# Layer 2 of a four-layer image network: the scan's states in PSUM, its decays in SBUF

## The chip, the cores and the metric

The kernel runs on one core of a Trainium2 chip. The metric is device time in microseconds: 3410.98, the median of three runs (3406.53 to 3415.37). A change of about 0.3% (10 us) is the least that such runs can tell from none.

## The reference, cut to what matters

Four layers follow each other on four images of 128 channels and 64 x 64 pixels: attention (layer 0), two quantized 3 x 3 convolutions (layer 1), a selective scan (layer 2) and a second attention (layer 3). The change lies in layer 2, whose core is this recurrence over the 4096 pixels of an image:

```python
def step(h, inp):
    dt_t, B_t, C_t, x_t = inp
    dA = jnp.exp(dt_t[..., None] * A)
    dBx = dt_t[..., None] * B_t[:, None, :] * x_t[..., None]
    h = dA * h + dBx
    y = jnp.einsum('bdn,bn->bd', h, C_t)
    return (h, y)
```

There are 256 inner channels d and 16 states n per channel. B and C are shared by all channels, A is fixed for each channel and state. Afterwards y is multiplied by silu(z), brought back to 128 channels, normalized in groups, passed through silu and added to the input of the layer.

## The kernel before, in words

**Tiles and steps.** Channels lie on the 128 partitions, 256 of them as two halves. Pixels are taken in blocks of 512 (TB), eight blocks an image, so NG = 32 groups g in all. A group has 16 steps, one for each state n; a step is m = 16 g + n, and there are NM = 512. One step works on [128, 2, 512] float32 values:

- `fetches` (line 1080): SP loads bc, the rows of B and C for this state, spread over all partitions; three buffers, so it waits for the product with C three steps before.
- `decays` (line 1093, two chains, one a half): ScalarE computes da = exp(dt * A), 128 x 512, into one PSUM bank a half (tags da0 and da1 of the pool `ps_a`). Each has one buffer, so it waits for the scan that read the last one.
- `scans` (line 1119): VectorE multiplies ud = dt * x with B into hs (line 1126), then multiplies the hs of the step before, in place, with C (`readout`, lines 1114 to 1117, called at line 1131), then scans the two halves of hs in place (line 1134).
- `lasts` (line 1104): ScalarE copies the last column of hs to hlast (line 1109), from which the same state of the next block starts. The last of an image's eight groups has no such copy, so there are 448 of them.
- `additions` (line 1146): GpSimd adds hs to y (line 1151), and after the 16th step multiplies y with silu(z) (line 1155).

hs has three buffers in SBUF (line 1125). The two weight tiles of layer 1 use the same buffers at the start (line 289).

**Beside layer 2.** `preparation` makes dt, ud, x and silu(z) for a group (its VectorE instructions are at lines 982 to 990); `output` finishes a group and an image (statistics at line 1020); `convolutions` is layer 1 (VectorE at lines 804, 816, 833, 838 and 840). Both attentions are staged over four images: `energies`, `exponentials` and `products` keep TensorE and ScalarE at work during the scans; `high_low` (line 445), `finish0` (lines 694 and 705) and `finish3` (lines 735 and 765) have their VectorE work. In the last stage, layer 3 of the fourth image, when the scans are over, the sums of the attention's exponentials are formed by `accumulations` on VectorE (line 575) and `totals` on TensorE (line 578), which takes the two da banks in turn.

**What sets the order.** Nothing is scheduled by a compiler. Each function above is a generator that yields a planned operation (engine, planned duration, names of the marks it needs) and then issues its instructions. `Order.run` (line 115) takes, at each turn, the operation with the smallest planned start plus 0.15 times its rank from the table `RANKS` (line 52). `port=True` marks VectorE operations that the planner keeps apart from GpSimd's. The result is a fixed order on each engine and queue. The waits between engines do not come from the planner: the tile layer adds the semaphores that the use of the buffers asks for, on the instruction itself or, where there are several, as semaphore instructions ahead of it.

Of the kernel before, what the change touches and what calls it, by code (L numbers as in the profile page):

```python
# [8 lines left out]
F32 = mybir.dt.float32  # L9
# [11 lines left out]
P = 128  # L21
W = 64
N = W * W
TB = 512
NTB = N // TB
# [11 lines left out]
CB = 256  # L37
# [12 lines left out]


RANKS = {
    "layer1_weights": dict(SP=-5.3, ACT=9.6, DVE=17.6, PE=-7.5),
    "layer2_weights": dict(SP=11.2, ACT=5.6, DVE=13.0),
    "parts": dict(ACT=0.8),
    "first": dict(ACT=-1.6, DVE=-2.8, PE=-4.9),
    "convolutions": dict(ACT=2.0, DVE=4.4, PE=4.2),
    "preparation": dict(SP=16.0, PE=2.4, ACT=0.9, DVE=3.0),
    "output": dict(PE=3.0, ACT=0.0, DVE=1.7, SP=-3.8),
    "lasts": dict(ACT=-0.0),  # L60
    "energies": dict(PE=3.5),
    "exponentials": dict(ACT=1.4),
    "products": dict(PE=5.1),
    "decays": dict(ACT=0.8),
    "scans": dict(DVE=4.7),
    "additions": dict(POOL=9.6),
    "fetches": dict(SP=-17.0),
    "accumulations": dict(DVE=15.7),
    "totals": dict(PE=-1.0),
    "images": dict(SP=9.9),  # L70
    "high_low": dict(ACT=4.8, DVE=2.3),
    "copy": dict(ACT=2.5),
    "finish0": dict(DVE=2.9, ACT=-1.9, PE=-5.1),
    "stage_input": dict(SP=9.0),
    "residual": dict(SP=2.8),
    "finish3": dict(PE=4.1, DVE=3.8, ACT=3.2, SP=-14.6),
}


class Order:  # L80
# [25 lines left out]
    def mark(self, *key):  # L106
        self.marks[key] = self.end
# [70 lines left out]
def conv_seq_kernel(ctx: ExitStack, tc: tile.TileContext, i: dict, out: bass.AP):  # L178
    nc = tc.nc
# [106 lines left out]
    def layer1_weights(k):  # L286
        unit, dt = ((LEVELS, F32R), (LEVELS * LEVELS, FP8))[k - 1]
        yield op("SP", 0.3, lag=4.0)
        w = mam.tile([P, 2, TB], F32, tag="hs", name=f"w{k}", bufs=3)
        last = att.tile([P, TB], F32, tag="t", name=f"w{k}_8", bufs=1)[:, 0:P]  # L290
        ws = (flat(w), last)
        nc.sync.dma_start(out=ws[0], in_=i[f"L1_conv_w{k}T"][:, 0 : 8 * P])
        nc.sync.dma_start(out=ws[1], in_=i[f"L1_conv_w{k}T"][:, 8 * P : 9 * P])
        yield op("ACT", 1.3, table="exp")
        for t in ws:
            nc.scalar.activation(t, t, AF.Tanh)
        yield op("DVE", 1.4)
        mx = sml.tile([P, 2], F32, tag="wmx", name="wmx")
        for n, t in enumerate(ws):
            nc.vector.tensor_reduce(  # L300
                mx[:, n : n + 1], t, AX.X, ALU.max, apply_absolute_value=True
            )
        nc.vector.tensor_reduce(mx[:, 0:1], mx, AX.X, ALU.max)
        yield op("PE", 0.4, bank=True)
        pt = gtile("wmx_t")
        nc.tensor.transpose(pt[0:1, 0:P], mx[:, 0:1], ident)
        yield op("DVE", 0.3)
        m1 = sml.tile([1, 1], F32, tag="wm1", name="wm1")
        nc.vector.tensor_reduce(m1, pt[0:1, 0:P], AX.X, ALU.max)
        release()  # L310
        yield op("PE", 0.6, bank=True)
        pb = gtile("wmx_b")
        nc.tensor.matmul(pb[:, 0:1], lhsT=ones[0:1, :], rhs=m1, start=True, stop=True)
        yield op("DVE", 0.4)
        rec = sml.tile([P, 1], F32, tag="wrec", name="wrec")
        nc.vector.tensor_scalar_mul(rec, pb[:, 0:1], 2.0)
        release()
        nc.vector.reciprocal(rec, rec)
        yield op("DVE", 2.4)
        for t in ws:  # L320
            nc.vector.tensor_scalar(t, t, rec, 0.5, ALU.mult, ALU.add)
            nc.vector.tensor_scalar(t, t, LEVELS, MAGIC, ALU.mult, ALU.add)
            nc.vector.tensor_scalar(t, t, MAGIC, 2.0, ALU.subtract, ALU.mult)
        yield op("DVE", 1.1)
        wi = const.tile([P, len(TAPS), P], dt, tag=f"wint{k}", name=f"wint{k}")
        for n, (dy, dx) in enumerate(TAPS):
            t = 3 * dy + dx
            nc.vector.tensor_scalar_add(
                wi[:, n, :], ws[t // 8][:, t % 8 * P : (t % 8 + 1) * P], -LEVELS, saturate=False
            )  # L330
        wint.append(wi)
        yield op("ACT", 0.9, table="sqrt")
        s = const.tile([P, 1], F32, tag=f"bn_s{k}", name=f"bn_s{k}")
        sh = const.tile([P, 1], F32, tag=f"bn_b{k}", name=f"bn_b{k}")
        rsqrt(s, cols[f"L1_conv_var{k}"])
        yield op("DVE", 1.3)
        nc.vector.tensor_mul(s, s, cols[f"L1_conv_gamma{k}"])
        nc.vector.tensor_mul(sh, cols[f"L1_conv_mean{k}"], s)
        nc.vector.tensor_sub(sh, cols[f"L1_conv_beta{k}"], sh)
        nc.vector.tensor_scalar_mul(s, s, LEVELS / unit)  # L340
        nc.vector.tensor_scalar_mul(sh, sh, LEVELS)
        bn.append((s, sh))
        mark("w", k)
        if k == 1:
            order.add(layer1_weights(2))
# [43 lines left out]
        stages += [(3, b)] + ([(0, b + 3)] if b + 3 < B else [])  # L389
    NQ = NJ // 8  # L390
    NS = NCB * NQ
    accs, sss = {}, {}
    its, jts, vts, es, ps, uss = {}, {}, {}, {}, {}, {}

    def stage_input(s):
# [182 lines left out]
    def totals():  # L578
        mark("total", (len(stages) - 1) * NCB - 1)
        for k in range((len(stages) - 1) * NCB, len(stages) * NCB):  # L580
            need = [("da", NM - 1, h) for h in range(2)]
            if k >= (len(stages) - 1) * NCB + 2:
                need.append(("evicted", k - 2))
            yield op("PE", 0.45, ("acc", NQ * k + NQ - 1), *need, tiles="columns")
            sss[k] = ss = ps_a.tile([P, TB], F32, tag=f"da{k % 2}", name="ss", bufs=1)[:, 0:CB]
            acc = accs.pop(k)
            for m in range(4):
                nc.tensor.matmul(
                    ss[32 * m : 32 * m + 32, :],
                    lhsT=ones[:, 0:32],  # L590
                    rhs=acc[:, m % 2, m // 2, :],
                    start=True,
                    stop=True,
                )
            mark("total", k)
# [267 lines left out]
    NG = NTB * B  # L863
    NM = NG * DS
    hlast = mam.tile([P, DS, 2], F32, tag="hlast", name="hlast")
    stats, live, bcs, das, hss = {}, {}, {}, {}, {}

    def pair(name, tag, bufs):
        return mam.tile([P, 2, TB], F32, tag=tag, name=name, bufs=bufs)
# [223 lines left out]
    def decays(h):  # L1093
        for m in range(NM):
            g, n = divmod(m, DS)
            need = [("s", m - 1, h)] if m else []
            yield op("ACT", 0.7, ("dt", g), *need, table="exp")
            das[m, h] = da = ps_a.tile([P, TB], F32, tag=f"da{h}", name="da", bufs=1)
            nc.scalar.activation(  # L1099
                da, live["in", g][0][:, h, :], AF.Exp, scale=amat[:, h, n : n + 1]  # L1100
            )
            mark("da", m, h)

    def lasts():
        for m in range(NM):
            g, n = divmod(m, DS)
            if g % NTB < NTB - 1:
                yield op("ACT", 0.2, ("s", m, 1))
                nc.scalar.copy(hlast[:, n, :], hss[m][:, :, TB - 1])  # L1109
                mark("last", m)  # L1110
            else:
                order.known(0.0, "last", m)

    def readout(m):
        hs = hss[m]
        nc.vector.tensor_mul(hs, hs, bcs.pop(m)[:, 1:2, :].to_broadcast([P, 2, TB]))  # L1116
        mark("c", m)

    def scans():
        for m in range(NM):  # L1120
            g, n = divmod(m, DS)
            need = [("add", m - 3)] if m > 2 else []
            yield op("DVE", 1.2, ("bc", m), ("ud", g), *need, port=True)
            ud = live["in", g][1]
            hss[m] = hs = pair("hs", "hs", 3)
            nc.vector.tensor_mul(hs, ud, bcs[m][:, 0:1, :].to_broadcast([P, 2, TB]))  # L1126
            if n == 0:
                mark("begun", g)
            if m:
                yield op("DVE", 1.13, ("last", m - 1), port=True)  # L1130
                readout(m - 1)
            for h in range(2):
                yield op("DVE", 1.19, ("da", m, h))
                nc.vector.tensor_tensor_scan(  # L1134
                    hs[:, h, :],
                    das.pop((m, h)),
                    hs[:, h, :],
                    hlast[:, n, h : h + 1] if g % NTB else 0.0,
                    ALU.mult,
                    ALU.add,  # L1140
                )
                mark("s", m, h)
        yield op("DVE", 1.13, ("last", NM - 1), port=True)
        readout(NM - 1)

    def additions():
        for m in range(NM):
# [541 lines left out]
```

## Time and profile before

| What | Before |
|---|---|
| Median of three runs | 3410.98 us |
| The profiled execution: its time, its span | 3404.14 us, 3402.3 us |
| TensorE matmul, busy | 3123.7 us, 92% |
| VectorE, busy | 3024.0 us, 89% |
| ScalarE, busy | 2573.9 us, 76% |
| GpSimd, busy | 1319.4 us, 39% |
| 500 to 1000 us: VectorE, TensorE, ScalarE busy | 491.45, 462.64, 402.65 us |
| 2000 to 2500 us: the same | 486.45, 456.03, 394.07 us |
| 3000 to 3402 us: the same | 226.96, 380.55, 221.73 us |
| Copies to hlast, line 1109, ScalarE | 448 of 189 ns |
| Decays, line 1099, ScalarE | 1024 of 690 ns |

A row of the profile's list of groups names the line, the engine, the operation, the tile written and the tiles read, the shapes and the count; then the busy time in us and the mean of one instruction in ns; then the idle time of that engine just before these instructions, and what ended it. In the list of slices, each digit is the busy share of a fortieth of the span, in tenths. A timeline line gives the start and duration in us first, and in brackets an idle time before it with the instruction that ended it. [...]

### The profile page before, as it was taken

How to read it: one execution, taken by the hardware profiler on the slowest of the kernel's cores; microseconds unless marked ns; L12 is line 12 of the kernel's file. 1: busy time of each engine (PE TensorE's matmuls, PEld its weight loads, DVE VectorE, ACT ScalarE, POOL GpSimd, SP SyncE). 2: the span in 40 equal slices, each digit the busy share in tenths (PEclk: the TensorE clock that was granted, in tenths of full speed). 3: DMA queues.
4: the chain of work that ended last, by engine and by line, in shares of the span. 5: the costliest groups of instructions: out<-in, count | busy, mean ns of one | idle time of the engine just before them, and what ended most of it. 6: DMA issues, size and time to landing. Idle time of an engine off the chain costs nothing.

```text
span 3402.3 us, 69611 instructions
## 1 busy us (share of the span) xinstructions
PE 3123.7 (92%) x29359; PEld 2249.8 (66%) x29359; DVE 3024.0 (89%) x2828; ACT 2573.9 (76%) x3899; POOL 1319.4 (39%) x565
## 2 busy tenths in 40 slices
PE   7999989999889999998988999999899899998998
PEld 5887768788678776555547888755455455555665
DVE  3199999999999999999999999999999999994554
ACT  4588877878788786878777888877788787865554
POOL 0044444444334444444434444444444445441000
PEclk9999999999999999999999999999999999999999
DMA  3033343333443334444443333444444444330000
GB/s 80 23 97 101 89 121 97 98 101 98 111 111 101 97 94 125 105 110 109 111 138 97 97 91 93 120 97 110 124 111 108 130 104 116 105 111 18 8 11 12
DMA packets 194179, 321.72 MB, mean 95 GB/s; under 512 B 44352, under 2 KB 46784, under 8 KB 193856
## 3 DMA queue, kind: packets, MB, share of 16 engines
q1 hardware_dynamic: 193568, 316.32, 35.1%
q8 instruction: 232, 3.80, 0.4%
q10 hardware_dynamic: 288, 0.85, 0.1%
q14 instruction: 91, 0.75, 0.1%
HBM read 300.35 MB, written 16.78 MB: 93 GB/s over the span
## 4 chain that ended last, share of the span: by engine, by line
DVE 50%; PE 29%; issue 10%; ACT 9%; DMA 2%; SPq 0%; DVEq 0%; ACTq 0%
DVE hs L1134 21%; DVE hs L1126 12%; DVE hs L1116 9%; PE e L535 8%; PE us L624 6%; PE us L615 6%; ACT p L553 2%; ACT da L1099 2%; PE us L643 1%; DMA bc<-bc_d 1%; DVE ud L984 1%; PE proj L458 1%; PE proj L500 1%; PE conv L777 1%; ACT L1099 1%
## 5 line engine op out<-in xcount | busy, mean ns | idle before, releaser
L1151 POOL TENSOR_TENSOR y<-y,hs 128x1024 f32<-128x1024 f32 x512 | 1216.7, 2376 | 1751.3 <-DVE hs L1116 1699.0
L553 ACT ACTIVATE p<-e 128x1024 f32<-128x1024 f32 x1024 | 1011.3, 1017 | 186.1 <-PE e L535 86.5
L1134 DVE TENSOR_TENSOR_SCAN hs<-da,hlast,hs 128x512 f32<-128x512 f32 x896 | 1098.8, 1263 | 8.2 <-ACT da L1099 8.1
L615 PE MATMUL us<-v,p 128*128 128x129 f32 x8192 | 1028.7, 281 | 16.4 <-ACT us L671 16.4
L615 PEld LDWEIGHTS us<-v,p 128*128 128x128 f32 x8192 | 959.6, 193 | 79.1 <-ACT us L671 22.7
L1099 ACT ACTIVATE da<-dt,late 128x512 f32<-128x512 f32 x1024 | 701.5, 690 | 249.8 <-DVE hs L1134 247.0
L1116 DVE TENSOR_TENSOR hs<-hs,bc 128x1024 f32<-128x1024 f32 x512 | 674.0, 1316 | 20.7 <-ACT hlast L1109 20.5
L1126 DVE TENSOR_TENSOR hs<-ud,bc 128x1024 f32<-128x1024 f32 x512 | 661.0, 1291 | 0.4
L535 PE MATMUL e<-it,v 64*128 64x256 f32 x4096 | 543.6, 401 | 64.3 <-ACT p L553 63.1
L624 PE MATMUL us<-p,v 128*32 128x256 f32 x8192 | 512.7, 386 | 22.0 <-ACT ss L680 22.0
L535 PEld LDWEIGHTS e<-it,v 64*128 64x128 f32 x4096 | 374.9, 190 | 222.6 <-ACT p L553 115.5
L624 PEld LDWEIGHTS us<-p,v 128*32 128x32 f32 x8192 | 244.8, 110 | 243.6 <-issue 70.3
L535 PE MATMUL e<-it,j 64*128 64x256 f32 x2048 | 222.4, 319 | 42.4 <-ACT p L553 39.2
L535 PEld LDWEIGHTS e<-it,j 64*128 64x128 f32 x2048 | 146.1, 187 | 127.3 <-ACT p L553 67.4
L643 PE MATMUL us<-p,ones 128*32 128x256 f32 x3072 | 204.3, 383 | 0.0
L575 DVE TENSOR_TENSOR acc<-p,acc 128x1024 f32<-128x1024 f32 x96 | 117.4, 1223 | 60.4 <-ACT p L553 56.1
L1109 ACT COPY hlast<-hs 128x2 f32<-128x2 f32 x448 | 84.8, 189 | 102.3 <-DVE hs L1134 93.5
L1134 DVE TENSOR_TENSOR_SCAN hs<-da,hs 128x512 f32<-128x512 f32 x128 | 149.4, 1203 | 0.9 <-ACT da L1099 0.8
L643 PEld LDWEIGHTS us<-p,ones 128*32 128x32 f32 x3072 | 89.5, 110 | 81.2 <-issue 32.6
L875 PEld LDWEIGHTS <-w 128*128 128x128 bf16 x576 | 53.4, 99 | 88.0 <-issue 47.3
L875 PE MATMUL xh<-x,w 128*128 128x512 fp8e4 x384 | 93.6, 380 | 8.5 <-ACT sz L898 5.8
L1155 POOL TENSOR_TENSOR y<-y,sz 128x1024 f32<-128x1024 f32 x32 | 100.1, 3127 | 2.5
(173 smaller groups left out, 2532.3 us busy)
## 6 DMA issues: line engine op xcount, KB each, us to landing
bc<-bc_d SPq DMA_DIRECT2D x512, 512.0 KB, 4.8
x_in<-in_x SPq DMA_DIRECT2D x16, 512.0 KB, 7.5
xpad<-in_x SPq DMA_DIRECT2D x32, 256.0 KB, 4.2
x_d<-yo SPq DMA_DIRECT2D x24, 256.0 KB, 2.9
x_in<-x_d SPq DMA_DIRECT2D x12, 512.0 KB, 7.3
o<-x_d SPq DMA_DIRECT2D x24, 256.0 KB, 5.3
out<-o SPq DMA_DIRECT2D x24, 256.0 KB, 2.5
bc_d<-xd SPq DMA_DIRECT2D x64, 32.0 KB, 4.2
```

Of the source, the lines that this page charges most:

```text
L535: nc.tensor.matmul(e[h][:, k % 2, k // 4, :], lhsT=jts[s][row : row + D3, col : col + P], rhs=its[s][row : row + D3, c * CB : (c + 1) * CB ...
L553: nc.scalar.activation(p, es[t][h], AF.Exp)
L575: nc.vector.tensor_add(accs[k], ps[t, h], other)
L615: nc.tensor.matmul(us[:, r, 0:VP], lhsT=ps[t, h][:, k % 2, k // 4, r * P : (r + 1) * P], rhs=vts[s][:, 8 * q + k, :], start=q == 0 and k = ...
L624: nc.tensor.matmul(us[m : m + 32, 0, :], lhsT=vts[s][:, 8 * q + k, m % D3 : m % D3 + 32], rhs=ps[t, h][:, k % 2, k // 4, :], start=q == 0 ...
L643: nc.tensor.matmul(us[32 * m : 32 * m + 32, 1, :], lhsT=ones[:, 0:32], rhs=term, start=False, stop=q == NQ - 1 and k >= len(terms) - 4,)
L875: nc.tensor.matmul(g, lhsT=w3[:, k // len(rhs), lhs[k % len(rhs)] : lhs[k % len(rhs)] + P], rhs=x[:, rhs[k % len(rhs)]], start=(k == 0), s ...
L1099: nc.scalar.activation(da, live["in", g][0][:, h, :], AF.Exp, scale=amat[:, h, n : n + 1])
L1116: nc.vector.tensor_mul(hs, hs, bcs.pop(m)[:, 1:2, :].to_broadcast([P, 2, TB]))
L1126: nc.vector.tensor_mul(hs, ud, bcs[m][:, 0:1, :].to_broadcast([P, 2, TB]))
L1134: nc.vector.tensor_tensor_scan(hs[:, h, :], das.pop((m, h)), hs[:, h, :], hlast[:, n, h : h + 1] if g % NTB else 0.0, ALU.mult, ALU.add,)
L1151: nc.gpsimd.tensor_tensor(y, y, hss.pop(m), ALU.add)
```

## The change

The states are computed in a PSUM pair h (two banks, one buffer), where the decays were; the decays go to SBUF. The product with C reads h and writes a tile hs in SBUF, of which there are now two, and GpSimd reads that. The product with C of step m-1 is issued ahead of the product with B of step m, because h has one buffer. In the plan, the product with B now needs the copy to hlast of the step before, the product with C needs only the addition two steps back in the same buffer, and it no longer has `port=True`. The totals of the last stage take h's two banks, as one tile for two of them. The ranks are different ones throughout, so the order on all engines and queues is another.

```diff
@@ RANKS
-    "layer1_weights": dict(SP=-5.3, ACT=9.6, DVE=17.6, PE=-7.5),
+    "layer1_weights": dict(SP=-9.7, ACT=1.4, DVE=18.8, PE=-17.8),
...
-    "lasts": dict(ACT=-0.0),
-    "exponentials": dict(ACT=1.4),
-    "decays": dict(ACT=0.8),
-    "scans": dict(DVE=4.7),
-    "additions": dict(POOL=9.6),
-    "fetches": dict(SP=-17.0),
+    "lasts": dict(ACT=-0.0),
+    "exponentials": dict(ACT=1.6),
+    "decays": dict(ACT=0.8),
+    "scans": dict(DVE=4.5),
+    "additions": dict(POOL=10.5),
+    "fetches": dict(SP=-12.1),
...
@@ layer1_weights
-        w = mam.tile([P, 2, TB], F32, tag="hs", name=f"w{k}", bufs=3)
+        w = mam.tile([P, 2, TB], F32, tag="hs", name=f"w{k}", bufs=2)
@@ totals
-            need = [("da", NM - 1, h) for h in range(2)]
+            need = [("c", NM - 1)]
             if k >= (len(stages) - 1) * NCB + 2:
-                need.append(("evicted", k - 2))
+                need.append(("evicted", k - (1 if k % 2 == 0 else 2)))
             yield op("PE", 0.45, ("acc", NQ * k + NQ - 1), *need, tiles="columns")
-            sss[k] = ss = ps_a.tile([P, TB], F32, tag=f"da{k % 2}", name="ss", bufs=1)[:, 0:CB]
+            if k % 2 == 0:
+                pairs[:] = [ps_a.tile([P, 2, TB], F32, tag="h", name="ss", bufs=1)]
+            sss[k] = ss = pairs[0][:, k % 2, 0:CB]
@@ decays
-            das[m, h] = da = ps_a.tile([P, TB], F32, tag=f"da{h}", name="da", bufs=1)
+            das[m, h] = da = mam.tile([P, TB], F32, tag=f"da{h}", name="da", bufs=1)
@@ lasts
-                nc.scalar.copy(hlast[:, n, :], hss[m][:, :, TB - 1])
+                nc.scalar.copy(hlast[:, n, :], states.pop(m)[:, :, TB - 1])
@@ readout and scans
-    def readout(m):
-        hs = hss[m]
-        nc.vector.tensor_mul(hs, hs, bcs.pop(m)[:, 1:2, :].to_broadcast([P, 2, TB]))
-        mark("c", m)
-
     def scans():
-        for m in range(NM):
+        for m in range(NM + 1):
             g, n = divmod(m, DS)
-            need = [("add", m - 3)] if m > 2 else []
+            if m:
+                need = [("add", m - 3)] if m > 2 else []
+                yield op("DVE", 1.15, *need)
+                hss[m - 1] = hs = pair("hs", "hs", 2)
+                nc.vector.tensor_mul(hs, h, bcs.pop(m - 1)[:, 1:2, :].to_broadcast([P, 2, TB]))
+                mark("c", m - 1)
+            if m == NM:
+                return
+            need = [("last", m - 1)] if m else []
             yield op("DVE", 1.2, ("bc", m), ("ud", g), *need, port=True)
             ud = live["in", g][1]
-            hss[m] = hs = pair("hs", "hs", 3)
-            nc.vector.tensor_mul(hs, ud, bcs[m][:, 0:1, :].to_broadcast([P, 2, TB]))
+            states[m] = h = ps_a.tile([P, 2, TB], F32, tag="h", name="h", bufs=1)
+            nc.vector.tensor_mul(h, ud, bcs[m][:, 0:1, :].to_broadcast([P, 2, TB]))
             if n == 0:
                 mark("begun", g)
-            if m:
-                yield op("DVE", 1.13, ("last", m - 1), port=True)
-                readout(m - 1)
-            for h in range(2):
-                yield op("DVE", 1.19, ("da", m, h))
+            for k in range(2):
+                yield op("DVE", 1.19, ("da", m, k))
                 nc.vector.tensor_tensor_scan(
-                    hs[:, h, :],
-                    das.pop((m, h)),
-                    hs[:, h, :],
-                    hlast[:, n, h : h + 1] if g % NTB else 0.0,
+                    h[:, k, :],
+                    das.pop((m, k)),
+                    h[:, k, :],
+                    hlast[:, n, k : k + 1] if g % NTB else 0.0,
                     ALU.mult,
                     ALU.add,
                 )
-                mark("s", m, h)
-        yield op("DVE", 1.13, ("last", NM - 1), port=True)
-        readout(NM - 1)
+                mark("s", m, k)
```

More of the change, by code (lines that the diff above doesn't have):

```diff
@@ L52 @@
 RANKS = {
-    "layer1_weights": dict(SP=-5.3, ACT=9.6, DVE=17.6, PE=-7.5),
[L54 to L59, printed above, removed]
+    "layer1_weights": dict(SP=-9.7, ACT=1.4, DVE=18.8, PE=-17.8),
+    "layer2_weights": dict(SP=-11.3, ACT=16.9, DVE=-3.7),
+    "parts": dict(ACT=0.4),
+    "first": dict(ACT=-10.8, DVE=-1.6, PE=-4.3),
+    "convolutions": dict(ACT=1.9, DVE=3.4, PE=4.9),
+    "preparation": dict(SP=18.8, PE=3.0, ACT=0.9, DVE=1.7),
+    "output": dict(PE=3.7, ACT=0.4, DVE=2.9, SP=20),
     "lasts": dict(ACT=-0.0),
-    "energies": dict(PE=3.5),
-    "exponentials": dict(ACT=1.4),
-    "products": dict(PE=5.1),
+    "energies": dict(PE=3.8),
+    "exponentials": dict(ACT=1.6),
+    "products": dict(PE=5.0),
     "decays": dict(ACT=0.8),
-    "scans": dict(DVE=4.7),
-    "additions": dict(POOL=9.6),
-    "fetches": dict(SP=-17.0),
[L68 to L76, printed above, removed]
+    "scans": dict(DVE=4.5),
+    "additions": dict(POOL=10.5),
+    "fetches": dict(SP=-12.1),
+    "accumulations": dict(DVE=18.1),
+    "totals": dict(PE=-8.7),
+    "images": dict(SP=-0.2),
+    "high_low": dict(ACT=0.3, DVE=1.1),
+    "copy": dict(ACT=0.6),
+    "finish0": dict(DVE=3.4, ACT=-20, PE=-1.0),
+    "stage_input": dict(SP=20),
+    "residual": dict(SP=10.2),
+    "finish3": dict(PE=4.2, DVE=4.0, ACT=4.5, SP=7.7),
 }
@@ L391, in conv_seq_kernel @@
     NS = NCB * NQ
-    accs, sss = {}, {}
+    accs, sss, pairs = {}, {}, []
     its, jts, vts, es, ps, uss = {}, {}, {}, {}, {}, {}
@@ L865, in conv_seq_kernel @@
     hlast = mam.tile([P, DS, 2], F32, tag="hlast", name="hlast")
-    stats, live, bcs, das, hss = {}, {}, {}, {}, {}
+    stats, live, bcs, das, hss, states = {}, {}, {}, {}, {}, {}
     def pair(name, tag, bufs):
```

## The prediction

> **What bounds the kernel now.** First the page: busy shares by slice, then the chain, then the costliest groups.
>
> ```profile
> DVE  3199999999999999999999999999999999994554
> ...
> DVE 50%; PE 29%; issue 10%; ACT 9%; DMA 2%; SPq 0%; DVEq 0%; ACTq 0%
> ...
> L1151 POOL TENSOR_TENSOR y<-y,hs 128x1024 f32<-128x1024 f32 x512 | 1216.7, 2376 | 1751.3 <-DVE hs L1116 1699.0
> ...
> L1134 DVE TENSOR_TENSOR_SCAN hs<-da,hlast,hs 128x512 f32<-128x512 f32 x896 | 1098.8, 1263 | 8.2 <-ACT da L1099 8.1
> ...
> L1116 DVE TENSOR_TENSOR hs<-hs,bc 128x1024 f32<-128x1024 f32 x512 | 674.0, 1316 | 20.7 <-ACT hlast L1109 20.5
> L1126 DVE TENSOR_TENSOR hs<-ud,bc 128x1024 f32<-128x1024 f32 x512 | 661.0, 1291 | 0.4
> ```
>
> VectorE is full from the second slice to the 35th: the busy table by stretches gives 97 to 98% from 500 to 3000 us. The first product with B starts at 172 us, the last product with C at 3076 us; behind it stands about 320 us of the last layer-3 stage, where PE leads. So what a layer-2 step costs VectorE, times 512 steps, moves the end directly. PE (92% busy over the span) and ScalarE (76%) have room if VectorE slows down, none to speak of if it speeds up.
>
> One step, from the timeline:
>
> ```profile
> 1515.04 1.21 DVE L1116 TENSOR_TENSOR hs<-hs,bc 128x1024 f32<-128x1024 f32 x1
> ...
> 1516.20 2.46 DVE L1134 TENSOR_TENSOR_SCAN hs<-da,hlast,hs 128x512 f32<-128x512 f32 x2
> 1516.39 2.35 POOL L1151 TENSOR_TENSOR y<-y,hs 128x1024 f32<-128x1024 f32 x1 [2.36 <-DVE hs L1116]
> ...
> 1518.57 1.26 DVE L1126 TENSOR_TENSOR hs<-ud,bc 128x1024 f32<-128x1024 f32 x1
> 1518.69 0.19 ACT L1109 COPY hlast<-hs 128x2 f32<-128x2 f32 x1
> ...
> 1519.75 1.21 DVE L1116 TENSOR_TENSOR hs<-hs,bc 128x1024 f32<-128x1024 f32 x1
> ```
>
> C to C is 4.71 us. Each instruction starts about 0.08 us before its predecessor's recorded end, since none reads what the one before it wrote: between the two scans and their product with C stands the next product with B. The copy to hlast (L1109) runs under that B product, the addition on GpSimd under the scans. Median start-to-start times over the trace, with nothing between: scan to scan 1.194, scan to B 1.175, B to C 1.215, C to scan 1.135, together 4.72 us.
>
> What an instruction costs that does wait for the VectorE instruction in front of it:
>
> ```profile
> 873.56 1.22 DVE L986 TENSOR_TENSOR dt<-dt,ud 128x1024 f32<-128x1024 f32 x1
> 874.82 1.23 DVE L990 TENSOR_TENSOR ud<-dt,xc 128x1024 f32<-128x1024 f32 x1
> 875.97 1.28 DVE L445 SCALAR_TENSOR_TENSOR it<-proj,early,h 128x1024 fp32r<-128x1024 f32 x1
> ```
>
> L990 needs L986 and starts 0.034 us after its end (median of all such pairs with that wait alone); L445 needs nothing of L990 and starts 0.08 before its end. Where the instruction has a second wait, so that the VectorE one is a semaphore instruction of its own, the gap is 0.104 (L575 on L575, second of a pair, no idle engine in front).
>
> And what GpSimd does to a VectorE product:
>
> ```profile
> 2021.46 2.42 POOL L1155 TENSOR_TENSOR y<-y,sz 128x1024 f32<-128x1024 f32 x1
> 2021.58 3.38 DVE L1126 TENSOR_TENSOR hs<-ud,bc 128x1024 f32<-128x1024 f32 x1
> ```
>
> The product starts second and ends 1.08 us after GpSimd (2024.96 against 2023.88); free, it takes 1.21.
>
> [...] L445 takes 1274 ns on 1024 and 739 on 512 elements, so 535 per 512; L986 from SBUF, 1225 less 535, is 690, and L765, with one PSUM input, has 678.
>
> **The change part by part.** VectorE's order becomes C(m-1), B(m), scan, scan, on one PSUM pair h. The order of the built program, with the instruction that each semaphore value stands for, shows:
>
> 1. Every VectorE instruction of a step waits for the one in front of it: C for the scan, B for C (h is overwritten), the first scan for B, the second for the first. Before, none did.
> 2. In 338 of 448 steps C also waits for the copy to hlast, both being reads of h; the copy has lost its cover. In 108 the copy stands behind C and waits for it; of these 105 products with B wait for the copy.
> 3. The addition waits for C as before, but C is now directly followed by B, which has two SBUF inputs; C itself has one.
>
> Cost per step; scan 1.271 and 1.252, products 1.225 when they wait (L986):
> - Scan to scan 1.271 + 0.104 = 1.375; C to B 1.225 + 0.034 = 1.259; B to scan 1.225 + 0.034, some with a second wait, 1.27.
> - 338 steps, C behind the copy: the copy starts 0.034 after the scan, takes 0.19, and C starts 0.102 later (ScalarE to VectorE is 0.032 on the instruction itself, 0.07 more for the second wait as in L575). ScalarE is often late: in the trace of before the copy starts at 0.035 in the median, at 0.29 in the mean; the late ones are likeliest the 108, so I take 0.1 here. 1.252 + 0.326 + 0.1 = 1.678. Step: 5.58, +0.86. B starts 0.034 after C, the addition 0.145 after C (median in the trace of before), so B is first and the addition waits, then lies under the scans. 338 x 0.86 = 291 us.
> - 105 steps, copy behind C: B can start 0.034 + 0.19 + 0.032 = 0.26 after C, the addition starts at 0.145 and is first: B ends at 0.145 + 2.37 + 1.08 = 3.60 after C. Step: 1.375 + 1.356 + 1.225 + 3.60 + 0.034 = 7.59, +2.87. 105 x 2.87 = 301 us.
> - The other 69: 1.375 + 1.356 + 1.259 + 1.27 = 5.26, +0.54: 37 us.
> - Foreign VectorE work between C and B, in some 32 steps long enough[...] (L705, L765, L1020, L445 of before), lets the addition in first: about 1.7 each, +54. Foreign work between scan and C (110 steps) hides the wait there, 0.37 each, and elsewhere about 13 in all: -54.
> - Gained: of the 512 C and 512 B, 28 were blocked (3.3 us, 2.1 more than free) by y*sz; C no longer contends, and y*sz, which follows the last addition, would now hold a B by some 0.3: -50. Idle time at the copy (20.5) falls under the new wait: -20.
>
> Sum: 291 + 301 + 37 + 54 - 54 - 50 - 20 = +559.
>
> At nothing, with ends: VectorE's writes into PSUM (B and both scans) are in no row. A gain cannot be excluded; [...] I take 0, as for PSUM reads. Decays into SBUF: +0.026 (716 of L994 against 690) x 1024 = 27 us of ScalarE, hidden by the 2.5 us and more between a scan and the same half's next one; uncovered, 27. Moving C releases bc earlier against B: SP's fetch has two steps, 10 us, for a landing of 4.8; nothing, and B alone would wait if SP's queue held it. Two hs instead of three: C waits for the addition two before, finished a step earlier. Totals in one pair wait for the copy of some 16 us before: nothing. The ranks reorder all queues; with VectorE the bound, PE's and ScalarE's order hides behind it; the head (172) and tail (320) may shift, +-20.
>
> The profiled execution has a span of 3402.3 and took 3404.1; 3404 + 559 = 3963. The median of the runs shown, 3411, is 7 above it: within my rounding; I say 3965.
>
> **Rivals.**
> - B is first even in the 105 steps. For: if its claim starts at dispatch, not at its wait's end. Against: every blocked case in the trace goes by start. 3965 - 105 x 2.34 = 3720.
> - The addition is first everywhere, 338 x 2.3 more: 4740. Against it: 0.034 before 0.145. It decides if B is held 0.11 longer than L986's kind, say by its DMA semaphore.
> - Faster: [...] Gain 50 at y*sz, 0.08 x 512 = 41 at B's start (1.291 down to 1.21), 20 at the copy[...]; PE, busy 3124 us and never without some idle time, would stop it half way: 3300. It needs gaps behind VectorE waits on PSUM under about -0.03 us, and the copy out of C's way; L986 and the waits in the program speak against it.
>
> **How the numbers follow.** Forecast 0.77 (own range 3840 to 4100[...]), first rival 0.12, second 0.06, third 0.05. The range takes in the first rival: 3700 to 4100. A measurement of this kernel tells 0.3% (10 us) from no change; faster 0.04, same 0.02, slower 0.94.
>
> **What would show it.** B's mean at some 1.7 to 1.8 us with about 140 of 512 over 3; the addition's mean over 3 us where it waits for B; C idle behind hlast about 0.35 in 338 steps; gaps of 0.1 between scans; VectorE's share of idle time up, PE's too. Wrong if the copy doesn't precede C in the waits, if B's mean stays under 1.3, or if scans change by over 0.07 each.

## The result and the profile after

| | Before | After |
|---|---|---|
| Median (range) | 3411.22 us (3406.53 to 3415.37) | 3995.07 us (3993.62 to 3995.46) |
| Profiled execution: time, span | 3404.14, 3402.3 us | 3995.42, 3993.5 us |
| VectorE busy, idle in the span | 3024.0, 378 us | 3443.6, 550 us |
| TensorE matmul busy | 3123.7 us, 92% | 3310.1 us, 83% |
| First product with B to the end of the last product with C | 2905 us | 3512 us |

The changed kernel takes 1.171 times as long (95% interval 1.169 to 1.173; four runs of each). Profile against profile it is +591 us, where the prediction's sum said +559. The whole difference lies in the stretch of the 512 steps, with the other work between them (+607); the head and the tail became 16 shorter.

The page of the changed kernel: the slices and engine shares of the chain, then the groups of the step.

```profile
DVE  3499999999989999999989999999999899998455
...
DVE 70%; PE 15%; ACT 7%; issue 5%; DMA 1%; DVEq 0%; POOL 0%; SPq 0%; ACTq 0%; POOLq 0%
...
L1151 POOL TENSOR_TENSOR y<-y,hs 128x1024 f32<-128x1024 f32 x512 | 1560.4, 3048 | 2023.0 <-DVE hs L1123 1940.2
L1136 DVE TENSOR_TENSOR_SCAN h<-da,hlast,h 128x512 f32<-128x512 f32 x896 | 1153.8, 1288 | 72.5 <-ACT da L1101 9.2
...
L1131 DVE TENSOR_TENSOR h<-ud,bc 128x1024 f32<-128x1024 f32 x512 | 915.6, 1788 | 35.1 <-ACT hlast L1111 22.9
...
L1123 DVE TENSOR_TENSOR hs<-h,bc 128x1024 f32<-128x1024 f32 x512 | 626.1, 1223 | 110.9 <-ACT hlast L1111 93.4
```

VectorE still sets the time, now with a larger share of the chain (70% for 50%). The product with B (L1131) went from 1291 to 1788 ns: not a slower instruction but a mixture. 137 of the 512 take more than 2 us (3.29 on average), a free one 1.233. The product with C (L1123) went from 1316 to 1223 ns, so it is free of GpSimd, but VectorE now stands idle in front of it: 110.9 us for 20.7, most of it for the copy to hlast. The addition (L1151) went from 2376 to 3048 ns: it is mostly second now. The scans became 1288 for 1263 ns, with 72.5 us idle in front of them for 8.2.

A step in which the copy is ahead of C, from the changed kernel's timeline (start, duration, in brackets the idle time before):

```profile
1815.04 1.23 DVE L1131 TENSOR_TENSOR h<-ud,bc 128x1024 f32<-128x1024 f32 x1
1815.15 3.35 POOL L1151 TENSOR_TENSOR y<-y,hs 128x1024 f32<-128x1024 f32 x1 [5.47 <-DVE hs L1123]
1816.31 2.68 DVE L1136 TENSOR_TENSOR_SCAN h<-da,hlast,h 128x512 f32<-128x512 f32 x2
...
1819.02 0.16 ACT L1111 COPY hlast<-h 128x2 f32<-128x2 f32 x1 [0.61 <-DVE h L1136]
1819.28 1.23 DVE L1123 TENSOR_TENSOR hs<-h,bc 128x1024 f32<-128x1024 f32 x1 [0.30 <-ACT hlast L1111]
1820.54 1.23 DVE L1131 TENSOR_TENSOR h<-ud,bc 128x1024 f32<-128x1024 f32 x1
```

Where before each start in a step lay 0.08 us ahead of the predecessor's end, none in this step does: 1.23 after 1815.04 is 1816.27, and the scans start at 1816.31; they end at 1818.99, the copy runs from 1819.02 to 1819.18, and C starts at 1819.28. B starts first and the addition, 0.11 later, lasts 3.35 instead of the 2.35 us that it takes when it is first (the next step below), beside the scans. B to B is 5.50 us.

A step with the copy behind C:

```profile
1559.08 1.23 DVE L1123 TENSOR_TENSOR hs<-h,bc 128x1024 f32<-128x1024 f32 x1
1560.34 0.16 ACT L1111 COPY hlast<-h 128x2 f32<-128x2 f32 x1 [1.42 <-DVE hs L1123]
1560.45 2.35 POOL L1151 TENSOR_TENSOR y<-y,hs 128x1024 f32<-128x1024 f32 x1 [5.35 <-DVE hs L1123]
1560.53 3.36 DVE L1131 TENSOR_TENSOR h<-ud,bc 128x1024 f32<-128x1024 f32 x1 [0.23 <-ACT hlast L1111]
```

Here B waits until the copy has ended, 0.23 us. In that time the addition starts, 0.08 us ahead of B, and B ends 1.09 us after it: the recorded 3.36 us, against 1.23 of a free B, take in the time that B was held. Those 0.08 us cost 2.1 us.

### The profile page after: what moved, and what is told of

It reads as the page before. It is cut to its first block, busy times and chain, and to the rows that moved or that the text cites. A ratio compares the mean times of both kernels' runs of the same rounds, so it can differ in the third digit from the quotient of the medians.

```text
span 3993.5 us, 70512 instructions
## 1 busy us (share of the span) xinstructions
PE 3310.1 (83%) x29359; PEld 2349.8 (59%) x29359; DVE 3443.6 (86%) x2828; ACT 2584.5 (65%) x3894; POOL 1649.0 (41%) x565
## 4 chain that ended last, share of the span: by engine, by line
DVE 70%; PE 15%; ACT 7%; issue 5%; DMA 1%; DVEq 0%; POOL 0%; SPq 0%; ACTq 0%; POOLq 0%
DVE h L1136 29%; DVE h L1131 21%; DVE hs L1123 13%; PE e L535 5%; PE us L626 4%; PE us L617 3%; ACT hlast L1111 1%; DVE ud L986 1%; ACT da L1101 1%; ACT p L553 1%; DVE y L984 1%; PE proj L458 1%; DVE dt L988 1%; DVE q L835 1%; DVE q L840 1%
## 5 line engine op out<-in xcount | busy, mean ns | idle before, releaser
L1151 POOL TENSOR_TENSOR y<-y,hs 128x1024 f32<-128x1024 f32 x512 | 1560.4, 3048 | 2023.0 <-DVE hs L1123 1940.2
L1136 DVE TENSOR_TENSOR_SCAN h<-da,hlast,h 128x512 f32<-128x512 f32 x896 | 1153.8, 1288 | 72.5 <-ACT da L1101 9.2
L1101 ACT ACTIVATE da<-dt,late 128x512 f32<-128x512 f32 x1024 | 732.0, 722 | 622.1 <-DVE h L1136 578.4
L617 PE MATMUL us<-v,p 128*128 128x129 f32 x8192 | 1075.5, 289 | 42.0 <-ACT us L673 39.2
L617 PEld LDWEIGHTS us<-v,p 128*128 128x128 f32 x8192 | 1009.7, 201 | 103.7 <-ACT us L673 46.6
L1131 DVE TENSOR_TENSOR h<-ud,bc 128x1024 f32<-128x1024 f32 x512 | 915.6, 1788 | 35.1 <-ACT hlast L1111 22.9
L1123 DVE TENSOR_TENSOR hs<-h,bc 128x1024 f32<-128x1024 f32 x512 | 626.1, 1223 | 110.9 <-ACT hlast L1111 93.4
L1111 ACT COPY hlast<-h 128x2 f32<-128x2 f32 x448 | 71.5, 160 | 323.7 <-DVE h L1136 194.2
L1136 DVE TENSOR_TENSOR_SCAN h<-da,h 128x512 f32<-128x512 f32 x128 | 157.0, 1226 | 10.5 <-ACT da L1101 1.5
L575 DVE TENSOR_TENSOR acc<-p,acc 128x1024 f32<-128x1024 f32 x96 | 117.4, 1223 | 52.4 <-ACT p L553 48.2
L965 PE MATMUL dt_ps<-xd,late 128*128 128x256 f32 x256 | 72.3, 406 | 18.6 <-ACT dt L975 13.1
```

Source lines behind the costliest of these rows:

```text
L575: nc.vector.tensor_add(accs[k], ps[t, h], other)
L617: nc.tensor.matmul(us[:, r, 0:VP], lhsT=ps[t, h][:, k % 2, k // 4, r * P : (r + 1) * P], rhs=vts[s][:, 8 * q + k, :], start=q == 0 and k = ...
L1101: nc.scalar.activation(da, live["in", g][0][:, h, :], AF.Exp, scale=amat[:, h, n : n + 1])
L1123: nc.vector.tensor_mul(hs, h, bcs.pop(m - 1)[:, 1:2, :].to_broadcast([P, 2, TB]))
L1131: nc.vector.tensor_mul(h, ud, bcs[m][:, 0:1, :].to_broadcast([P, 2, TB]))
L1136: nc.vector.tensor_tensor_scan(h[:, k, :], das.pop((m, k)), h[:, k, :], hlast[:, n, k : k + 1] if g % NTB else 0.0, ALU.mult, ALU.add,)
```

## The experiments

The theory was the prediction's: three things come with the states in PSUM. The states' pair makes every VectorE instruction wait for the one before; the copy to hlast and the product with C, both reads of the pair, are kept apart (by 0.10 us in the first step above); and where the copy is second, B is late and the addition is ahead of it. The rivals were that the accesses to PSUM are dear in themselves, that the other ranks alone cost the time, and that GpSimd is ahead nearly everywhere. The times of e1, e2, e3, e5, e6 and e8 are of one execution each. Apart from e6, which is read as no difference, they lie over 100 us from the changed kernel, whose four runs spread over 2 us.

**e1: the copy always ahead of C.** An edit of the plan on the changed kernel; nothing of the computation changes. The plan is made anew, so other places in the queues can move with it.

```diff
                 need = [("add", m - 3)] if m > 2 else []
-                yield op("DVE", 1.15, *need)
+                yield op("DVE", 1.15, ("last", m - 1), *need)
                 hss[m - 1] = hs = pair("hs", "hs", 2)
```

> The changed kernel, with the product with C planned behind the copy to hlast, so that none of the 448 copies stands behind its C (108 did). Theory (a copy behind C lets GpSimd's addition in ahead of the product with B): the 105 products with B that took 3.3 us fall to 1.24, each such step gains 2.06 less some 0.3 of waiting for the copy, about 190 us: 3805, range 3770 to 3840; products with B over 2 us fall from 137 to about 35. Rival (PSUM as a place is slow, or the new order is): within 20 us of 3995.

Measured: 3864.77 us, 131 less than the changed kernel. Its groups:

```profile
L1123 DVE TENSOR_TENSOR hs<-h,bc 128x1024 f32<-128x1024 f32 x512 | 625.9, 1223 | 178.6 <-ACT hlast L1111 173.1
L1131 DVE TENSOR_TENSOR h<-ud,bc 128x1024 f32<-128x1024 f32 x512 | 676.8, 1322 | 15.9
```

Of the 137 long products with B, 22 are left, and B's busy time fell by 239 us (915.6 to 676.8). So the held products are a matter of which of two reads goes first, as the theory says. But the time fell by 131 only: the wait moved to C, whose idle time rose by 68 (110.9 to 178.6). The rest of VectorE's idle time rose by 22 and its other work by 18. Part of the reason shows in the trace: the copies that had been second now start 0.27 us after their scan on average, the others 0.19, so ScalarE comes to them later, and VectorE stands idle for 0.46 us before their C and for 0.36 us before the others'. The theory had the direction and put the wait too low: the run is 25 us above the expected range.

**e2: the copy always behind C.** The other end of the same choice.

```diff
-                yield op("ACT", 0.2, ("s", m, 1))
+                yield op("ACT", 0.2, ("s", m, 1), ("c", m))
                 nc.scalar.copy(hlast[:, n, :], states.pop(m)[:, :, TB - 1])
```

> The changed kernel, with every copy to hlast planned behind its product with C, so that about 436 products with B wait for the copy, not 105. Theory (the addition starts 0.145 us after C, B 0.23 us after it, so B is held for the whole addition): 331 more products of 3.3 us, each step about 2.0 longer, +660 us: 4655, range 4500 to 4750; GpSimd's additions fall to a mean near 2.4 us, as none waits. Rival (PSUM as a place, or the order): within 40 us of 3995.

Measured: 4539.55 us, in the range. The groups:

```profile
L1151 POOL TENSOR_TENSOR y<-y,hs 128x1024 f32<-128x1024 f32 x512 | 1271.1, 2483 | 2844.7 <-DVE hs L1123 2748.7
L1131 DVE TENSOR_TENSOR h<-ud,bc 128x1024 f32<-128x1024 f32 x512 | 1505.3, 2940 | 129.4 <-ACT hlast L1111 125.5
```

429 of 512 products with B take over 2 us, and the addition is back at 2483 ns, from 3048: the two have changed places. One read's place in a queue moves this kernel from 3865 to 4540 us.

**e3: the states in SBUF.** The changed kernel with its order, its ranks, its one state pair and its separate tile for the product; only the state pair is in SBUF and the decays are back in PSUM (with them, not shown, the totals of the last stage).

```diff
-            das[m, h] = da = mam.tile([P, TB], F32, tag=f"da{h}", name="da", bufs=1)
+            das[m, h] = da = ps_a.tile([P, TB], F32, tag=f"da{h}", name="da", bufs=1)
...
-            states[m] = h = ps_a.tile([P, 2, TB], F32, tag="h", name="h", bufs=1)
+            states[m] = h = pair("h", "hst", 1)
```

> The changed kernel's order and its separate tile for GpSimd, with the single state tile h in SBUF and the decays back in PSUM. Built, the product with C no longer waits for the copy and the second scan no longer waits for the first; B waits for C and for the copy, its VectorE wait a semaphore instruction. Theory: a step is 1.19 + 1.36 + 1.33 + 1.26 = 5.15 us, +0.43 on the kernel before, 512 times, plus 20 to 50 for foreign work that lets the addition in: 3640, range 3580 to 3720. If B, now 0.104 us behind C, loses to the addition at 0.145 after all, 4600 or more. Rival (the order C, B, scan, scan is what costs, not the place): within 40 us of 3995. Rival (PSUM accesses are slow): scans of 1.26 and below instead of 1.289, and that is all the difference, 3960.

Measured: 3677.51 us, in the range. The groups, whose lines lie two lower in this kernel:

```profile
L1134 DVE TENSOR_TENSOR_SCAN h<-da,hlast,h 128x512 f32<-128x512 f32 x896 | 1103.5, 1270 | 30.8 <-ACT da L1099 10.5
L1129 DVE TENSOR_TENSOR h<-ud,bc 128x1024 f32<-128x1024 f32 x512 | 719.9, 1406 | 45.3 <-ACT hlast L1109 8.7
L1121 DVE TENSOR_TENSOR hs<-h,bc 128x1024 f32<-128x1024 f32 x512 | 652.3, 1274 | 43.2 <-DVE h L1134 1.4
```

In a step of its timeline the copy runs beside C:

```profile
1509.81 0.19 ACT L1109 COPY hlast<-h 128x2 f32<-128x2 f32 x1 [0.48 <-DVE h L1134]
1509.88 1.23 DVE L1121 TENSOR_TENSOR hs<-h,bc 128x1024 f32<-128x1024 f32 x1
1511.19 1.23 DVE L1129 TENSOR_TENSOR h<-ud,bc 128x1024 f32<-128x1024 f32 x1
```

C starts 0.07 after the copy, while the copy is running, and the second scan of a pair starts 0.08 before the end of the first again. So the wait between copy and C, and that between the two scans, belong to the states being in PSUM. In the theory this is narrower than stated: the waits from scan to C (0.104) and from C to B (0.091) are left in this kernel, and come of the single pair and of C's place, not of PSUM. The placement, of states and decays together, is worth 3995.07 - 3677.51 = 318 us of the loss; the order with a single pair, a separate product and the new ranks 3677.51 - 3411.22 = 266. Part of the 266 is again GpSimd's: 49 products with B and 14 with C take over 2 us here, where before it was 28 of both.

**e5: the copy on VectorE.** The changed kernel, the copy between the scans and C on the same engine, so that it keeps its place in PSUM but needs no second engine.

```diff
-                yield op("ACT", 0.2, ("s", m, 1))
-                nc.scalar.copy(hlast[:, n, :], states.pop(m)[:, :, TB - 1])
+                yield op("DVE", 0.1, ("s", m, 1))
+                nc.vector.tensor_copy(hlast[:, n, :], states.pop(m)[:, :, TB - 1])
...
-    "lasts": dict(ACT=-0.0),
+    "lasts": dict(DVE=-20.0),
```

Besides, C needs ("last", m - 1), as in e1.

> The changed kernel, with the copy to hlast on VectorE, between the second scan and the product with C, so that no wait for ScalarE is left in a step. Theory: scan to copy 0.034, the copy 0.16 less 0.08 of overlap, then C, so 0.12 in place of the 0.45 us in front of C that the run with all copies ahead of C had in its 442 steps; that run's 3865 less 146, plus 22 for first scans that get a second wait: 3740, range 3690 to 3790. Products with B over 2 us: about 35. Rival (PSUM accesses or the order make the step long): no gain on 3865.

Measured: 3757.53 us, in the range. Its timeline:

```profile
1504.18 2.68 DVE L1136 TENSOR_TENSOR_SCAN h<-da,hlast,h 128x512 f32<-128x512 f32 x2
...
1506.90 0.16 DVE L1111 COPY hlast<-h 128x2 f32<-128x2 f32 x1
...
1506.97 1.21 DVE L1123 TENSOR_TENSOR hs<-h,bc 128x1024 f32<-128x1024 f32 x1
1508.22 1.23 DVE L1131 TENSOR_TENSOR h<-ud,bc 128x1024 f32<-128x1024 f32 x1
```

Copy and C, both reads of the pair on one engine, overlap by 0.09 us (1506.90 + 0.16 against 1506.97). The bound engine does 448 more instructions, 71 us of them, and the kernel is 238 us faster than the changed one: an instruction of 0.16 us is cheaper on the bound engine than a wait for it on another. Not all of the 238 us belongs to the engine, though: 131 of them come of having every copy ahead of C, as in e1, and against e1 the copy on VectorE gains 107 (3864.77 - 3757.53).

**e8: without the additions.** The changed kernel without the 512 additions on GpSimd.

```diff
-            nc.gpsimd.tensor_tensor(y, y, hss.pop(m), ALU.add)
-            mark("add", m)
+            hss.pop(m)
+            mark("add", m)
```

> The changed kernel without the 512 additions on GpSimd: the scan's result stays out of y, so that the output lacks it. Theory: no addition can hold a product with B; 105 x 2.06 = 216 us for those behind the copy and about 55 for those behind foreign work go: 3725, range 3690 to 3770, products with B over 2 us below 15. The waits for the copy and the gaps stay: the idle time of C and the start-to-start times are as in the changed kernel. Rival (the additions are harmless, the waits are all): within 30 us of 3995.

Measured: 3621.69 us, 374 less than the changed kernel, 68 below the range. The groups of the two products:

```profile
L1123 DVE TENSOR_TENSOR hs<-h,bc 128x1024 f32<-128x1024 f32 x512 | 625.8, 1222 | 89.9 <-ACT hlast L1111 84.1
L1131 DVE TENSOR_TENSOR h<-ud,bc 128x1024 f32<-128x1024 f32 x512 | 638.5, 1247 | 37.7 <-ACT hlast L1111 25.6
```

B gained 277 us (915.6 to 638.5), which was expected, and B keeps its wait for the copy (25.6), so it was GpSimd that made it long. Two things were not expected. C's wait behind the copy is 0.23 instead of 0.30. In the changed kernel the trace has 267 products with C with the wait for the addition on the instruction itself and the one for the copy as a semaphore instruction ahead of it; here, without an addition to wait for, 273 have the wait for the copy on the instruction itself:

```profile
1501.91 0.16 ACT L1111 COPY hlast<-h 128x2 f32<-128x2 f32 x1 [0.61 <-DVE h L1136]
1502.11 1.23 DVE L1123 TENSOR_TENSOR hs<-h,bc 128x1024 f32<-128x1024 f32 x1 [0.23 <-ACT hlast L1111]
```

And VectorE work outside the step became shorter. The same group (shapes kept apart), first in the changed kernel, then in e8:

```profile
L986 DVE TENSOR_TENSOR ud<-ud,y 128x1024 f32<-128x1024 f32 x32 | 59.6, 1862 | 1.1
```

```profile
L986 DVE TENSOR_TENSOR ud<-ud,y 128x1024 f32<-128x1024 f32 x32 | 39.2, 1225 | 1.1
```

In the changed kernel this product, which has nothing to do with h, is held for 0.64 us on average. With its neighbours L984 (50.5 to 39.8), L988 (45.3 to 39.2), L835 (32.0 to 21.7), L840 (23.9 to 13.7) and L818 (22.8 to 12.6) that is 68 us. Before the change, all of these but L988 were held too, but less.

**e4: the kernel before with the ranks of the changed one.** Nothing else differs.

> The kernel before with nothing changed but the table of ranks, which is the changed kernel's. Theory (VectorE's step sets the time, the order beside it little): within 25 us of 3411. Rival (the other order on the queues is what costs): a good part of the 584 us, 3600 or more.

Measured: 3486.11 us (3482.68 to 3494.86), 1.021 times before (1.019 to 1.023). A miss: 25 at most were expected, and it is 73 to 75.

```profile
L1134 DVE TENSOR_TENSOR_SCAN hs<-da,hlast,hs 128x512 f32<-128x512 f32 x896 | 1098.8, 1263 | 31.7 <-ACT da L1099 31.7
```

Its instructions are as long as before, to the digit (1098.8, 1263). VectorE's idle time went from 378 to 459 us: the scans wait 31.7 us for decays where they waited 8.2, L694 waits 59.4 us where it waited 38.6. With VectorE near the bound, ScalarE's order did not hide behind it.

**e6: the changed kernel with the ranks of the one before.**

> The changed kernel with the table of ranks of the kernel before. Built, 75 copies stand behind their C, not 108. Theory: 30 fewer held products with B, -62 us; on the other side up to the 75 us that strange ranks cost the kernel before: 3930 to 4010. Rival (the ranks are a good part of the 584 us): 3920 or less with as many held products.

Measured: 3998.21 us, against 3995.07. With the old ranks fewer copies stand behind C (75 for 108), so B is shorter (841.6 us for 915.6), but VectorE's idle time is 626 us for 550, so nothing is left of it. So the ranks do not explain the loss: the change without its ranks loses the same.

**e7: the kernel before with y * silu(z) on VectorE.** 28 products with B or C of the kernel before take over 2 us; the expectation put this down to this GpSimd instruction. Here VectorE does it itself.

```diff
-                yield op("POOL", 2.4, ("sz", g))
-                nc.gpsimd.tensor_tensor(y, y, live.pop(("sz", g)), ALU.mult)
+                yield op("DVE", 1.15, ("sz", g), port=True)
+                nc.vector.tensor_mul(y, y, live.pop(("sz", g)))
```

> The kernel before with the gating y*silu(z) of each group on VectorE, not on GpSimd. Theory: in the kernel before 28 products with B or C are held 2.1 us by it, 59 us; on VectorE it costs 32 x 1.14 = 37: 3390, range 3375 to 3405. Rival (VectorE is full, so 32 more instructions cost their time and the held products were hidden): 3430 to 3450.

Measured: 3422.7 us (eight runs, 3418.19 to 3426.12), 1.0034 times before (1.0023 to 1.0045). A miss. The first half came true: no product with B or C takes over 2 us any more, C fell from 1316 to 1214 ns, B from 1291 to 1272, and the stretch from the first B to the last C from 2905 to 2890 us. But what follows took 358 us instead of 325. VectorE's waits from 3000 us on, first before, then e7:

```profile
DVE rall L735 <- PE sc L726: 25.2, 10, 2.8
```

```profile
DVE rall L735 <- PE sc L726: 71.2, 9, 49.5
```

Between 3100 and 3402 us TensorE was busy for 300.5 of 302 us in e7, and for 290.7 before; VectorE once waited 49.5 us for it. TensorE was behind when the scans ended: from 3100 us to the end it had 3752 matmuls left in e7, 3477 before. From there on it set the time. So the kernel before had two bounds close together, and 15 us gained on VectorE met the other one. Whether TensorE was behind only because VectorE was earlier, or also because the plan put its work in another order, was not tried.

No version here beats the kernel before.

## Why the prediction was right

The mechanism and its three parts stand; the sum, +559, was 32 us below the +591 of the profiles. Term by term ("clean" steps have no other work in them; their times are medians of the trace, against 4.72 before):

| Term of the prediction | Predicted | Measured |
|---|---|---|
| Steps with the copy ahead of C | 338 x 0.86 = 291 | 5.50 us a step: 338 x 0.78 = 264 |
| Copy behind C, B held | 105 x 2.87 = 301 | 7.63 us a step: 102 x 2.91 = 297 |
| Other steps | 69 x 0.54 = 37 | 5.38 us a step: 72 x 0.66 = 48 |
| Other work between C and B lets the addition in | +54 | 137 - 102 = 35 further long B; 73 (915.6 less 512 free ones and the 102) |
| C and B no longer held by y * silu(z) | -50 | -48 in C's busy time |
| Other work that hides the wait for the copy | -54 | 238 of 338 steps show the wait (0.376 on average); 100 x 0.376 + 13 is about -50 |
| Other VectorE work held by longer additions | not in the sum | about +46 |
| Head and tail | 0 (+-20) | -16 |

With the -20 for the idle time at the copy as predicted, the right column gives 594, 3 above what the profiles differ by. That it comes so close is partly luck: the steps are medians, and the 238 waits for the copy alone are 0.08 us longer in the mean (0.376 for 0.296), 19 us in all.

- "Every VectorE instruction of a step waits for the one in front of it": right, with its prices. C to B 0.034, B to the first scan 0.036, scan to scan 0.104 (it was -0.077). e3 shows whose waits they are: the one between the scans goes with PSUM, those around C stay.
- "In 338 of 448 steps C also waits for the copy": right. The gap from scan to C is 0.296 in the median where 0.326 was worked out, since the copy out of PSUM takes 0.160 and not 0.19. Its mean of 0.376 is near the 0.43 with the lateness of 0.1. e3 and e5 remove this wait in two ways.
- "The addition waits for C, but C is now directly followed by B": right. The place rule of the prediction, who starts first is first, held on both sides: B behind the copy started 0.226 after C, lost to the addition at 0.145 and took 3.34 on average; free, it started at 0.034 and won. This excludes the rival of B first even in the 105 steps (3720), and that of the addition first everywhere (4740). The second was one position in ScalarE's queue away, though: e2, where the addition is first nearly everywhere, takes 4540.
- PSUM accesses at nothing: nearly right. B written to PSUM takes 1.233 where a free product in SBUF (L986 of the kernel before) takes 1.225; C from PSUM takes what it takes otherwise. The scans, as means, became longer by 0.025 (0.023 for those without hlast), 25 us over 1024 scans; their busy time on the page rose by 63 us, since before the two of a pair overlapped and now they don't. The sum priced a pair at 1.271 + 1.252 and the medians are 1.289 each, so these 25 us or so came on top of it; they are inside the clean steps. So for products no run here shows a price of PSUM beyond 0.01 us, in line with the prediction's ground for it (L765 with a PSUM input takes 678 ns, L986 from SBUF, brought to the same 512 elements by an estimate from L445's 1274 and 739 ns, 690); for the scans, which read and write it, the runs show 0.025 us.
- Ranks +-20: the outcome was right for this kernel (e6: 3 us), but by luck: in e6 VectorE's busy time is 73 us shorter and its idle time 76 longer, and the two cancel. The reason was not right. "PE's and ScalarE's order hides behind" VectorE is refuted by e4, where the same ranks cost 75 us.
- The rival "faster", 3300 with TensorE as the stop, had too much room: e7's 15 us on VectorE were all lost to TensorE.

The term that was mis-sized is the missing one: the prediction followed the addition against B and left out whom else it holds. Before, most additions ran beside scans and took 2.38 us. In the changed kernel 355 start behind B and take 3.33, about a microsecond longer, which reaches into other work. The groups L984, L986, L988, L835, L818, L840 and L1064 take 260.1 us together and took 213.6 before, +46; e8 shows the additions as the cause. With these 46 the prediction's sum would be 605, 14 above the 591.

Two of the held lines have a single input in SBUF: L840 takes 745 ns in the changed kernel and 427 without the additions, L818 takes 815 and 450. The prediction took C, with its one input in SBUF, as free of GpSimd; that holds for C (1223 ns with the additions, 1222 without), and one input in SBUF did not keep these two free. What sets them apart from C, no run here shows. The prediction also took L705, L765, L1020 and L445 of before as work that lets the addition in ahead of B, by its author's estimate: in the changed kernel 27 of the 137 long products with B follow directly on these lines (L707, L767, L1022 and L445 there).

Open: whether the wait between the two scans would go if each half had a tile of its own in PSUM was not tried, nor the states in PSUM or the decays in SBUF each on its own. That B, where it is first, holds the additions is read from the timelines and from e2, where they are short again.

## What to carry to other kernels

Before a tile that two engines read is moved to PSUM, list its readers: reads that ran beside each other in SBUF (e3: C starts 0.07 us after the copy's start) were put one after the other here (0.10 after its end), and the second of them paid 0.3 us a step or, through what slipped in between, 2.1. Where the bound engine waits for a short instruction of another engine, price it on the bound engine itself (e5: 71 us more work, and 107 us faster than e1, which has the same copies ahead of C on ScalarE). And when an instruction is taken off one contention, ask which neighbour inherits it, and when the bound engine gains, whether the next one (here TensorE at 92%) lets any of it through.

## What was not expected of the hardware

- Which of two waits is the separate semaphore instruction matters. C of the changed kernel has the wait for the copy there and starts 0.102 us after the copy's end (median of 238). C in e8 has it on the instruction itself and starts 0.033 after (240). B behind its copy, in the changed kernel, has a second wait as well, for the landing of bc, but the copy's is on B itself, and B starts 0.032 after (99). So a second wait as such cost nothing; the 0.07 us came where the wait that ended last was the separate one.
- A copy of 128x2 on ScalarE takes 0.160 us from PSUM and 0.189 from SBUF (e3 has it in SBUF, the changed kernel in PSUM).
- TensorE's mean granted clock was mostly lower where TensorE was less busy: 0.979 before (busy 92%), 0.957 in e3 (87%), 0.931 in the changed kernel (83%), 0.874 in e2 (75%). The share alone does not give it: e7 is as busy as the kernel before (92%) and has 0.970. The mean is made of two values, 1.0 and 0.5, in these traces; the kernel before has 29 stretches at 0.5, 144 us together, the changed one 100, 552 us. In the 3.4 us, the length of the shortest of them, ahead of such a stretch TensorE was busy for 37% of the time in the median before and for 29% in the changed kernel. So it went with TensorE's gaps; no run tried its cause.
